# Layer 3 of a four-layer network: norm factors applied in pairs, disc units and spread statistics rescheduled, and a separate tail for the last image

## The chip, the cores and the metric

One core of a Trainium2 chip runs the whole network in one launch. The time is device microseconds (us) of that launch; three runs of the kernel before are known, and one further execution was recorded by the hardware profiler.

## What is computed

The input is `x`, 8 images of 32 x 32 tokens with 256 channels, float32. Four layers follow one another, each `x = x + f(group_norm(x))`. Only the fourth, layer 3, is touched (and one preparation step for it that is issued during layer 2):

```python
qkv = silu(x @ w_qkv.T); q, k, v = split(qkv, 3)
q, k = rope(rms_norm(q)), rope(rms_norm(k))          # per head, 8 heads of 32 channels
wp = silu(x @ w_wp.T + b_wp); width_raw, sharp_raw = split(wp, 2)
width = sigmoid(width_raw) * max_dist + 0.5; sharp = sigmoid(sharp_raw) * 9.5 + 0.5
scores = einsum(q, k_win) * 32**-0.5                 # a 7 x 7 window round each token
soft_mask = sigmoid((width - rel_dist) * sharp)      # the "soft disc"
attn = softmax(scores - (1 - soft_mask) * 10000)
out = rms_norm(einsum(attn, v_win), w_on)            # over all 256 channels
return silu((out + v) @ w_out.T)
```

(The rotation's angle depends on the head alone and is the same for q and k, so it cancels in the scores, and no rope step stands in the kernel.)

## The kernel before, in words

**Tiling.** Layer 3 works channel-major: 128 channels (four heads) in the partitions, the 1024 tokens of an image along the free axis. An image `b` has two channel halves `c`; one such half is a *chunk* `J = 2b + c`, 16 in all. A chunk is worked off in 8 *groups*, each two 8 x 8 blocks of queries against a window of 14 x 14 keys: 128 groups. The main loop (lines 2308 to 2333) runs over *steps* `n` from -4 to N + 2 with N = 128, and every step does one stage of several groups:

- `st.scores(n+3)`, TensorE (PE): 8 small matmuls into four PSUM tiles (L1692).
- `st.exps(n)`, ScalarE (ACT): four exponentials (L1715).
- `st.logits(n+3)`, VectorE (DVE): scores plus mask with the running minimum (L1705).
- `st.turn(n-2, i)`: PE transposes of the probabilities (L1733), DVE copies them out of PSUM (L1738).
- `soft(n+5)`, ACT: four tanh that make the soft disc (L2103); `masked(n+5)`, GpSimd (POOL): adds the hard window (L2110).
- `st.divide(n)`: reciprocal on DVE (L1722), product on POOL (L1723).
- `st.values(n-3)`: PE (L1749), then two DVE copies to the output tile `oT` (L1757).

**Order.** The order is written out by hand for PE, ACT, DVE and POOL (`manual_schedule`); each engine takes its instructions in that order, and SyncE (SP) issues the DMAs in it. All PSUM tiles come from one ring of 8 banks (`ring`, L1549), so a matmul into a new tile waits for the reader of the tile 8 places earlier.

**Fillers.** The rest of the layer is cut into units that `plan_chunk`, `plan_image` and the loop after L2251 give a due time in steps; `units(n)` emits those due, and `units(n + 0.5)` those of the half step. A unit may return a second part, kept in `later` and run by the next `finish()`. Due times relative to the chunk's first step 8J:

- `project` (L2042, silu with tanh at L2027): k at -12, -11.5, q at -11, -10.5, v at -7.5, -7. For k and q POOL squares the result (L2062).
- `roots` at -8: PE sums the squares of q and k per head, and for even J those of the attention output of image b - 2 (L2122, L2129), ACT loads another activation table (L2136) and takes Ln and Exp (L2137, L2138), which makes the reciprocal norm factors `fac[J]`; the next tanh loads the first table again.
- `head_scale` (L2144): one 32-row matmul spreads a factor over the channels, DVE multiplies (L2148); k at -6, -5.5, q at -5, -4.5.
- `in_strips` at -6 and `vturn` at -2, -1.5, -1, -0.5, 1.5: PE transposes v (L1766), ACT copies it from PSUM (L1771).

Relative to an image's first step 16b: statistics of the group norm at -23.5 to -22, `normed` at -13.5 and -13, `discs` (width and sharpness, L2075 to L2094, one chain over DVE and ACT) at -10 and -9.5; after the attention `tail_sq` (POOL, L2172) at 19 and 20, `tail_scale` (four 32-row matmuls, L2177, DVE L2181, POOL L2182) at 30 to 31.5, `output` (L2190, L2197, L2199, L2200) at 33.5, 39, 39.5 and 41.5, each with a `reload` of the residual three steps ahead. What is still due after the last step is emitted by the loop at L2334.

## Time and profile before

| what | us |
|---|---|
| three runs: median (lowest to highest) | 3300.57 (3299.59 to 3302.94) |
| the profiled execution: its time | 3305.0 |
| the profiled execution: span from first to last instruction | 3303.2 |
| layer 3 within the span: first projection to the end | about 2503 to 3303 |
| first exponential of group 0; of group 32; of group 112; end of the last | 2531.9; 2735.4; 3197.8; 3261.3 |
| last copy of an attention output (L1757) to the end of the span | 3272.95 to 3303.15 |

The span shares on the page are PE 96%, ACT 69%, DVE 66%, POOL 54% busy. "PEclk" is the clock granted to PE, 1.0 being full speed; "idle before" is what an engine waited ahead of an instruction, and the arrow names what ended the wait. A float32 matmul of the program appears as two PE instructions. L12 is line 12 of the kernel before.

### The profile page before, as it was taken

The page shows a single profiled execution, that of the slowest core. Times are in us where ns is not written, and L with a number is a line of the kernel's source. Part 1 is how long each engine was busy: PE and PEld are TensorE (multiplying, and loading weights), DVE is VectorE, ACT ScalarE, POOL GpSimd, SP SyncE. Part 2 cuts the span into 40 slices and gives each one's busy share as a digit, 9 for nine tenths or more (in the row PEclk, how much of TensorE's full clock was granted, in tenths as well). Part 3 has the DMA queues.
Part 4 walks back from the last instruction along what each step waited for, and adds up shares of the span by engine and source line. Part 5 has one row for each costly group of instructions (what it writes and reads, how often), then busy time and mean ns, then how long its engine had stood idle before and what let it go on. Part 6 is the DMA issues. An engine that isn't in the chain of part 4 may idle for free. (4 is left out here: it accounts for less than half of the span.)

```text
span 3303.2 us, 76346 instructions
## 1 busy us (share of the span) xinstructions
PE 3165.7 (96%) x30280; PEld 1638.2 (50%) x30280; DVE 2192.5 (66%) x5570; ACT 2278.5 (69%) x5066; POOL 1792.1 (54%) x1201
## 2 busy tenths in 40 slices
PE   7999999999998999899999999999998899999997
PEld 2323323323322444777777656666664555555554
DVE  4777777777785677565655546666664667777775
ACT  3667667667776567666555547677676878888885
POOL 4666666666663111344444445433436668788777
PEclk9999999999999999999999999999998879999999
DMA  3000000000011667787867630111111001110001
GB/s 142 1 26 10 17 26 1 26 26 1 26 39 57 235 233 260 208 206 204 182 192 205 182 138 28 66 41 40 53 55 44 2 14 40 34 37 30 27 27 62
DMA packets 139177, 267.92 MB, mean 81 GB/s; under 512 B 9218, under 2 KB 77700, under 8 KB 130500
## 3 DMA queue, kind: packets, MB, share of 16 engines
q1 hardware_dynamic: 132436, 242.67, 24.3%
q10 hardware_dynamic: 6384, 20.37, 1.8%
q8 instruction: 239, 3.92, 0.5%
q14 instruction: 118, 0.97, 0.1%
HBM read 177.81 MB, written 85.20 MB: 80 GB/s over the span
## 5 line engine op out<-in xcount | busy, mean ns | idle before, releaser
L694 DVE TENSOR_TENSOR e<-s,ret 128x1024 f32<-128x1024 f32 x512 | 602.1, 1217 | 174.4 <-PE s L688 171.9
L701 ACT ACTIVATE ea<-e 128x1024 f32<-128x1024 f32 x512 | 535.5, 1055 | 257.3 <-DVE e L694 234.9
L703 POOL TENSOR_TENSOR ea<-ea 128x1024 f32<-128x1024 f32 x128 | 304.1, 2376 | 284.9 <-ACT ea L701 216.9
L688 PE MATMUL s<-qk,qk 32*128 32x512 f32 x2048 | 302.1, 640 | 4.3 <-POOL qk L571 1.7
L1591 POOL TENSOR_TENSOR e<-e,su 128x616 f32<-128x616 f32 (+2 forms) x128 | 157.3, 1229 | 268.7 <-DVE su L1590 241.9
L740 PE MATMUL num<-e,v 128*32 128x512 f32 x2048 | 271.3, 595 | 0.0
L1738 DVE COPY pts<-pt 112x512 f32<-112x512 f32 x256 | 175.8, 687 | 137.5 <-PE pt L1733 135.7
L2103 ACT ACTIVATE e<-win,disc 128x196 f32<-128x196 f32 x512 | 239.5, 543 | 0.2
L1723 POOL TENSOR_TENSOR e<-e,su 128x784 f32<-128x784 f32 x128 | 191.4, 1495 | 87.9 <-DVE su L1722 62.0
L870 PE MATMUL up_ps<-x,wup 128*128 128x512 f32 x512 | 230.2, 604 | 4.0 <-POOL x L236 3.2
L1715 ACT ACTIVATE e<-e,mx 128x196 f32<-128x196 f32 x512 | 227.9, 453 | 0.0
L2110 POOL TENSOR_TENSOR e<-e,win 128x784 f32<-128x784 f32 x128 | 201.7, 1576 | 38.5 <-issue 31.6
L1282 POOL TENSOR_TENSOR decayed<-state,rb 128x520 f32<-128x520 f32 x48 | 50.8, 1058 | 304.2 <-PE sc L1215 112.7
L1586 ACT ACTIVATE e<-e,mx 128x154 f32<-128x154 f32 (+2 forms) x512 | 212.2, 425 | 0.0
L1086 ACT ACTIVATE d<-d,cols 128x128 f32<-128x128 f32 x512 | 163.9, 392 | 68.5 <-POOL d L1077 68.4
L713 PE MATMUL sm<-ea,ones 128*32 128x512 f32 x1536 | 208.8, 604 | 1.6 <-POOL ea L703 1.6
L897 DVE SCALAR_TENSOR_TENSOR cv<-xm,par,cv 128x512 f32<-128x512 f32 x192 | 144.7, 754 | 85.8 <-ACT cv L892 81.2
L2042 PE MATMUL qkv_ps<-xq,w 128*128 128x512 f32 x384 | 192.2, 627 | 1.2 <-ACT fac L2137 1.2
L1823 PE MATMUL qkv_ps<-x,w 128*128 128x512 f32 x384 | 182.7, 613 | 1.6 <-POOL x L236 1.6
L688 PEld LDWEIGHTS s<-qk,qk 32*128 32x128 f32 x2048 | 84.8, 182 | 197.2 <-issue 87.7
L1733 PEld LDWEIGHTS pt<-idg,e 128*112 128x112 f32 x1024 | 121.5, 140 | 122.5 <-issue 91.0
L1733 PE MATMUL pt<-idg,e 128*112 128x128 f32 x1024 | 166.5, 289 | 8.4 <-DVE oT L1757 3.1
(245 smaller groups left out, 6932.8 us busy)
## 6 DMA issues: line engine op xcount, KB each, us to landing
d<-l1rows SPq DMA_DIRECT2D x64, 512.0 KB
x<-x SPq DMA_DIRECT2D x25, 1024.0 KB
l1xm<-xm SPq DMA_DIRECT2D x16, 1024.0 KB
l1sz<-sz SPq DMA_DIRECT2D x16, 1024.0 KB
xv<-l1xm SPq DMA_DIRECT2D x32, 512.0 KB
l1xa<-xa SPq DMA_DIRECT2D x16, 1024.0 KB
xa<-l1xa SPq DMA_DIRECT2D x16, 1024.0 KB
rb<-l1rows SPq DMA_DIRECT2D x32, 512.0 KB
```

The source lines that it names most:

```text
L688: nc.tensor.matmul(s[:, j % 2], qk[b, 1, c][g, kb * P : (kb + 1) * P], qk[b, 0, c][g, h * HALF : (h + 1) * HALF], start=True, stop=True,)
L694: nc.vector.tensor_mul(e[n, i], s, m)
L701: nc.scalar.activation(ea[n, i], e[n, i], AF.Abs)
L703: nc.gpsimd.tensor_add(ea[n, i], ea[n, i], ea.pop((n - 1, i)))
L713: nc.tensor.matmul(acc["sm"][g, :], ones, two[j // 2][:, j % 2, :], start=kb == 0 and k == 0, stop=kb == 4 and k == 2,)
L740: nc.tensor.matmul(acc["num"][g, :], v[b][:, kb, vc], e[n, j // 2][:, j % 2, :], start=kb == 0, stop=kb == 7,)
L870: nc.tensor.matmul(ps, wup[:, kc, m * P : (m + 1) * P], seg(s)[:, kc], start=kc == 0, stop=kc == 1,)
L1586: self.nc.scalar.activation(p[:, j], p[:, j], AF.Exp, scale=-1.0, bias=mx[:, j : j + 1], accum_out=su[:, j : j + 1],)
L1715: self.nc.scalar.activation(e[:, j], e[:, j], AF.Exp, scale=-1.0, bias=mx[:, j : j + 1], accum_out=self.su[:, j : j + 1],)
L1733: self.nc.tensor.transpose(ps[: self.PART, at : at + P], self.tile(n)[:, 2 * i + j, k * self.PART : (k + 1) * self.PART], self.K.ident,)
L2103: nc.scalar.activation(e[:, j], win[:, 0], AF.Tanh, scale=disc[b][:, i, 8 + h : 9 + h], bias=disc[b][:, i, h : h + 1],)
L2110: nc.gpsimd.tensor_add(e, e, win[:, 1].unsqueeze(1).to_broadcast([P, 4, NWIN]))
```

## The change

All in layer 3:

- `head_scale` does both halves of k, or of q, in one unit: two 32-row matmuls one after the other into two PSUM tiles, the two products in the second part. Due at -6 (k) and -5 (q).
- `tail_scale` has one matmul per token half where it had one per half and channel half: the matrix of the matmul is now ones, and the weight `w_on` goes in as the per-partition scalar of the DVE instruction. Due at 27.5 and 28.5. Its constants come by two DMAs in the preparation step.
- The copy of the transposed v (`value_unit`) goes from ACT to DVE and into the second part.
- `discs` becomes a chain of five parts, one per `finish()`; due at -13, -12.5. `finish()` runs one part of every chain. `normed` at -15, statistics at -23.75 (two), -22.5, -21.5.
- v is projected at -8.5 and -8; `roots` comes after it in the same step.
- `exps(n+1)` stands where `exps(n)` stood. In every eighth step (`rooted`) `soft(n+5)` comes ahead of the units, and a `finish()` and a quarter step follow the logits.
- `output` runs by token half at 29.5, 30.5, 31, 31.5, and `reload` at 26.5, 27.5, 28, 30.5.
- The last image has a tail of its own (`last_tail`, due N + 3): PSUM takes `wo` times v first and `wo` times the normed output is added to it there, so no POOL addition of v; half of the squares are taken on ACT; the residual is the image itself, loaded whole at 16b + 6.

```diff
-        self.nc.scalar.copy(
+        return lambda: self.nc.vector.tensor_copy(
...
+        def root(ps, n):
+            r = wk.tile([P, HALF], F32, name="fac", bufs=2)
+            nc.scalar.preload_act_table_set("natural_log_exp_and_others")
+            nc.scalar.activation(r[:n], ps[:n], AF.Ln, bias=eps[:n])
+            nc.scalar.activation(r[:n], r[:n], AF.Exp, scale=-0.5)
+            return r
...
-        def head_scale(J, s, h):
-            g = slice(32 * (2 * s + h), 32 * (2 * s + h) + 32)
-            ps = st.ring("fac_ps")
-            nc.tensor.matmul(ps, spread[g, s], fac[J][g], start=True, stop=True)
+        def head_scale(J, s):
+            ps = [st.ring("fac_ps") for _ in range(2)]
+            for h in range(2):
+                g = slice(32 * (2 * s + h), 32 * (2 * s + h) + 32)
+                nc.tensor.matmul(ps[h], spread[g, s], fac[J][g], start=True, stop=True)
...
-            nc.tensor.matmul(ps, won[g, c], fac[J][g], start=True, stop=True)
+            nc.tensor.matmul(ps, ones[g], fac[J][g], start=True, stop=True)
             def rest():
-                d = st.o[b, c][:, hs]
-                nc.vector.tensor_mul(d, d, ps)
-                nc.gpsimd.tensor_add(d, d, vT[b, c][:, hs])
+                for c in range(2):
+                    d = st.o[b, c][:, hs]
+                    nc.vector.scalar_tensor_tensor(
+                        d, d, on[:, c : c + 1], ps, ALU.mult, ALU.mult)
+                    nc.gpsimd.tensor_add(d, d, vT[b, c][:, hs])
...
+        def last_tail(b):
+            ps = {}
+            def early(m):
+                for h in range(2):
+                    ps[m, h] = st.ring("out_ps")
+                    for kc in range(2):
+                        nc.tensor.matmul(ps[m, h], wo[:, kc, m * P : (m + 1) * P],
+                            vT[b, kc][:, h * HALF : (h + 1) * HALF],
+                            start=kc == 0, stop=False)
+            early(0)
+            sq, o = sqs["o", 1], st.o[b, 1]
+            nc.scalar.activation(sq[:, HALF:], o[:, HALF:], AF.Square)
+            sums = st.ring("ms_ps")
+            for c, h in ((0, 0), (0, 1), (1, 0), (1, 1)):
+                if c and h:
+                    early(1)
+                nc.tensor.matmul(sums[32 * h : 32 * h + 32], sel[:, 32:64], ...)
+            f = root(sums, 64)
+            for h in range(2):
+                fp = st.ring("fac_ps")
+                nc.tensor.matmul(fp, ones[g], f[g], start=True, stop=True)
+                for c in range(2):
+                    nc.vector.scalar_tensor_tensor(d, d, on[:, c : c + 1], fp, ALU.mult, ALU.mult)
+            for h in range(2):
+                for m in range(2):
+                    for kc in range(2):
+                        nc.tensor.matmul(ps[m, h], wo[...], st.o[b, kc][:, hs],
+                            start=False, stop=kc == 1)
+                    y = half_silu(p)
+                    nc.vector.scalar_tensor_tensor(y, y, 1.0, p, ALU.add, ALU.mult)
+                    e = nc.vector if m and h else nc.gpsimd
+                    e.tensor_add(r, r, y)       # r is the image, loaded again at 16b + 6
+                    nc.sync.dma_start(dst[...], r)
...
-                if 0 <= n < N:
-                    st.exps(n)
+                if 0 <= n + 1 < N:
+                    st.exps(n + 1)
+                rooted = n % 8 == 0
+                if rooted and 1 < n + 5 < N:
+                    soft(n + 5)
                 units(n)
                 if 0 <= n + 3 < N:
                     st.logits(n + 3)
+                if rooted:
+                    finish()
+                    units(n + 0.25)
                 if 0 <= n - 2 < N:
                     st.turn(n - 2, 0)
                 finish()
-                if 1 < n + 5 < N:
+                if not rooted and 1 < n + 5 < N:
                     soft(n + 5)
...
         def finish():
-            while later:
-                later.pop(0)()
+            due = later[:]
+            later[:] = [r for r in [f() for f in due] if callable(r)]
```

More of the change, by code (lines that the diff above doesn't have):

```diff
@@ L90, in shape_constants @@
     k["k_spread"] = (p[:, None] % 32 == p[None] // 32).astype(f)
+    k["k_one8"] = np.tile(p[:, None] % 32 == 8, (1, P)).astype(f)
     return {n: np.ascontiguousarray(v) for n, v in k.items()}
@@ L145, in layouts @@
     )
-    a["l3_on"] = i["L3_conv_w_on"].reshape(2, P)
+    a["l3_on"] = _cols(i["L3_conv_w_on"])
     a.update(shape_constants())
@@ L395, in factors @@
             )
-            nc.vector.memset(won, 0.0)
         def weight():
-            for h in range(2):
-                nc.sync.dma_start(
-                    self.won[32 * h + 8 : 32 * h + 9], a["l3_on"].unsqueeze(0)
-                )
+            nc.sync.dma_start(self.won[:, 0], a["k_one8"])
+            nc.sync.dma_start(self.won[:, 1, 0:2], a["l3_on"])
         return [loads, factors, weight]
@@ L1671, in __init__ @@
         super().__init__(K, wk, pp, pairs, n_img, ebufs)
-        self.slots, self.s = 20, {}
+        self.slots, self.s, self.su = 20, {}, {}
         shape = [P, 4, 2 * self.PART]
@@ L1712, in exps @@
         mx, e = self.mx.pop(n), self.prob(n)
-        self.su = self.wk.tile([P, 4], F32, name="su", bufs=4)
+        su = self.su[n] = self.wk.tile([P, 4], F32, name="su", bufs=4)
         for j in range(4):
@@ L1716, in exps @@
                 e[:, j], e[:, j], AF.Exp, scale=-1.0, bias=mx[:, j : j + 1],
-                accum_out=self.su[:, j : j + 1],
+                accum_out=su[:, j : j + 1],
             )
     def divide(self, n):
-        e = self.prob(n)
-        self.nc.vector.reciprocal(self.su, self.su)
-        self.nc.gpsimd.tensor_mul(e, e, self.su.unsqueeze(2).to_broadcast([P, 4, NWIN]))
+        e, su = self.prob(n), self.su.pop(n)
+        self.nc.vector.reciprocal(su, su)
+        self.nc.gpsimd.tensor_mul(e, e, su.unsqueeze(2).to_broadcast([P, 4, NWIN]))
     def turn(self, n, i):
@@ L1997, in layer3 @@
         K.ring = st.ring
-        bwp, sel, spread, won = first.bwp, first.sel, first.spread, first.won
+        bwp, sel, spread = first.bwp, first.sel, first.spread
+        ones, on = first.won[:, 0], first.won[:, 1, 0:2]
         wo, win, eps = first.wo, first.win, first.eps
@@ L2085, in rest, with silu, silu2, sigmoid @@
                 )
-                th = wk.tile([P, 4, 16], F32, name="dth")
-                nc.scalar.activation(th, d, AF.Tanh)
+                return silu
+            def silu():
+                th = wk.tile([P, 4, 16], F32, name="dth", bufs=2)
+                nc.scalar.activation(th, disc[b][:, 4 * u : 4 * u + 4, :], AF.Tanh)
+                return lambda: silu2(th)
+            def silu2(th):
+                d = disc[b][:, 4 * u : 4 * u + 4, :]
                 nc.vector.scalar_tensor_tensor(d, th, 1.0, d, ALU.add, ALU.mult)
+                return sigmoid
+            def sigmoid():
+                d = disc[b][:, 4 * u : 4 * u + 4, :]
                 nc.scalar.activation(d, d, AF.Tanh, scale=0.5)
+                return scales
+            def scales():
+                d = disc[b][:, 4 * u : 4 * u + 4, :]
                 wd, sp = d[:, :, 0:8], d[:, :, 8:16]
@@ L2133, in roots @@
                         )
-            n = P if heads else 64
-            r = wk.tile([P, HALF], F32, name="fac", bufs=2)
-            nc.scalar.preload_act_table_set("natural_log_exp_and_others")
-            nc.scalar.activation(r[:n], ps[:n], AF.Ln, bias=eps[:n])
-            nc.scalar.activation(r[:n], r[:n], AF.Exp, scale=-0.5)
-            fac[J] = r
-        def head_scale(J, s, h):
-            g = slice(32 * (2 * s + h), 32 * (2 * s + h) + 32)
-            ps = st.ring("fac_ps")
-            nc.tensor.matmul(ps, spread[g, s], fac[J][g], start=True, stop=True)
+            fac[J] = root(ps, P if heads else 64)
+        def head_scale(J, s):
[3 more added lines that the diff above has]
+                nc.tensor.matmul(ps[h], spread[g, s], fac[J][g], start=True, stop=True)
             def rest():
-                d = dest(J, s, h)
-                nc.vector.tensor_mul(d, d, part(ps))
+                for h in range(2):
+                    d = dest(J, s, h)
+                    nc.vector.tensor_mul(d, d, part(ps[h]))
             return rest
@@ L2166, in vturn, with tail_sq, tail_scale @@
                 st.v[b, c] = wk.tile([P, st.slots, P], F32, name="v", bufs=2)
-            st.value_unit(strips, st.v[b, c], u)
-        def tail_sq(b, c):
+            return st.value_unit(strips, st.v[b, c], u)
+        def tail_sq(b, c, n=L):
             sqs["o", c] = wk.tile([P, L], F32, name="sq", bufs=4)
-            nc.gpsimd.tensor_mul(sqs["o", c], st.o[b, c], st.o[b, c])
-        def tail_scale(J, b, c, h):
+            o = st.o[b, c][:, 0:n]
+            nc.gpsimd.tensor_mul(sqs["o", c][:, 0:n], o, o)
+        def tail_scale(J, b, h):
             g, hs = slice(32 * h, 32 * h + 32), slice(h * HALF, (h + 1) * HALF)
             ps = st.ring("fac_ps")
-            nc.tensor.matmul(ps, won[g, c], fac[J][g], start=True, stop=True)
+            nc.tensor.matmul(ps, ones[g], fac[J][g], start=True, stop=True)
             def rest():
-                d = st.o[b, c][:, hs]
-                nc.vector.tensor_mul(d, d, ps)
-                nc.gpsimd.tensor_add(d, d, vT[b, c][:, hs])
+                for c in range(2):
+                    d = st.o[b, c][:, hs]
+                    nc.vector.scalar_tensor_tensor(
+                        d, d, on[:, c : c + 1], ps, ALU.mult, ALU.mult
+                    )
+                    nc.gpsimd.tensor_add(d, d, vT[b, c][:, hs])
             return rest
@@ L2208, in reload @@
             nc.sync.dma_start(r, src[:, m, b * L + h * HALF : b * L + (h + 1) * HALF])
+        def last_tail(b):
[4 more added lines that the diff above has]
+                    for kc in range(2):
+                        nc.tensor.matmul(
+                            ps[m, h], wo[:, kc, m * P : (m + 1) * P],
+                            vT[b, kc][:, h * HALF : (h + 1) * HALF],
+                            start=kc == 0, stop=False,
+                        )
+            early(0)
[5 more added lines that the diff above has]
+                    early(1)
+                nc.tensor.matmul(
+                    sums[32 * h : 32 * h + 32], sel[:, 32:64],
+                    sqs["o", c][:, h * HALF : (h + 1) * HALF],
+                    start=c == 0, stop=c == 1, skip_group_check=True,
+                )
+            f = root(sums, 64)
+            for h in range(2):
+                hs = slice(h * HALF, (h + 1) * HALF)
+                fp = st.ring("fac_ps")
+                g = slice(32 * h, 32 * h + 32)
+                nc.tensor.matmul(fp, ones[g], f[g], start=True, stop=True)
+                for c in range(2):
+                    d = st.o[b, c][:, hs]
+                    nc.vector.scalar_tensor_tensor(
+                        d, d, on[:, c : c + 1], fp, ALU.mult, ALU.mult
+                    )
+            for h in range(2):
+                hs = slice(h * HALF, (h + 1) * HALF)
+                for m in range(2):
+                    p = ps[m, h]
+                    for kc in range(2):
+                        nc.tensor.matmul(
+                            p, wo[:, kc, m * P : (m + 1) * P], st.o[b, kc][:, hs],
+                            start=False, stop=kc == 1,
+                        )
+                    y = half_silu(p)
+                    nc.vector.scalar_tensor_tensor(y, y, 1.0, p, ALU.add, ALU.mult)
+                    r = x[b][:, m, hs]
+                    e = nc.vector if m and h else nc.gpsimd
+                    e.tensor_add(r, r, y)
+                    nc.sync.dma_start(
+                        dst[:, m, b * L + h * HALF : b * L + (h + 1) * HALF], r
+                    )
@@ L2219, in plan_chunk @@
                 fill.add(n - 12 + i / 2, lambda s=s, h=h: project(J, s, h))
-                fill.add(n - 6 + i / 2, lambda s=s, h=h: head_scale(J, s, h))
-            fill.add(n - 7.5, lambda: project(J, 2, 0))
-            fill.add(n - 7, lambda: project(J, 2, 1))
+            for s in range(2):
+                fill.add(n - 5 - s, lambda s=s: head_scale(J, s))
+            fill.add(n - 8.5, lambda: project(J, 2, 0))
+            fill.add(n - 8, lambda: project(J, 2, 1))
             fill.add(n - 6, lambda: in_strips(J))
@@ L2228, in plan_image @@
                 fill.add(n - 27.5, lambda: load(b))
+                ahead = (n - 23.75, n - 23.75, n - 22.5, n - 21.5)
                 for i in range(4):
                     fill.add(
-                        max(n - 23.5, -3) + i / 2,
+                        ahead[i] if b > 1 else -3 + i / 2,
                         lambda i=i: gn.stats(b, image_parts(x[b]), i),
@@ L2236, in plan_image @@
                 for c in range(2):
-                    fill.add(n - 13.5 + c / 2, lambda c=c: normed(b, c))
+                    fill.add(max(n - 15, 2) + c / 2, lambda c=c: normed(b, c))
                 for u in range(2):
-                    fill.add(n - 10 + u / 2, lambda u=u: discs(b, u))
+                    fill.add(max(n - 13, 4) + u / 2, lambda u=u: discs(b, u))
+            if b == n_img - 1:
+                fill.add(n + 6, lambda: load(b))
+                fill.add(n + 11, lambda: tail_sq(b, 0))
+                fill.add(N + 1.75, lambda: tail_sq(b, 1, HALF))
+                fill.add(N + 3, lambda: last_tail(b))
+                return
             for c in range(2):
                 fill.add(n + 19 + c, lambda c=c: tail_sq(b, c))
-                for h in range(2):
-                    fill.add(
-                        n + 30 + c + h / 2,
-                        lambda c=c, h=h: tail_scale(2 * b + 4, b, c, h),
-                    )
-            for i in range(4):
-                at = n + 32 + (1.5, 7, 7.5, 9.5)[i]
-                fill.add(at - 3, lambda i=i: reload(b, i // 2, i % 2))
-                fill.add(at, lambda i=i: output(b, i // 2, i % 2))
-        for J in range(2 * n_img + 3):
+                fill.add(n + 27.5 + c, lambda c=c: tail_scale(2 * b + 4, b, c))
+            for i in range(4):
+                h, m = divmod(i, 2)
+                fill.add(n + (26.5, 27.5, 28, 30.5)[i], lambda h=h, m=m: reload(b, m, h))
+                fill.add(n + (29.5, 30.5, 31, 31.5)[i], lambda h=h, m=m: output(b, m, h))
+        N = len(st.groups)
+        for J in range(2 * n_img + 1):
             b, c = divmod(J, 2)
             t = b - 2 if c == 0 and b >= 2 else None
+            if J < 2 * n_img:
+                plan_chunk(J)
             if J and (J < 2 * n_img or t is not None):
                 fill.add(8 * J - 8, lambda J=J, t=t: roots(J, t))
-            if J < 2 * n_img:
-                plan_chunk(J)
         for b in range(n_img):
@@ L2264, in layer3 @@
                 fill.add(at, lambda J=J, u=u: vturn(J, u))
-        N = len(st.groups)
         later = []
@@ L2274, in finish, with all_of @@
         def finish():
-            while later:
-                later.pop(0)()
+            due = later[:]
+            later[:] = [r for r in [f() for f in due] if callable(r)]
+        def all_of(*rests):
+            while rests:
+                rests = [r for r in [f() for f in rests] if callable(r)]
         def start():
@@ L2281, in start @@
             rest = [discs(0, 0), discs(0, 1), project(0, 1, 0)]
-            rest[0]()
-            rest[2]()
-            r = project(0, 1, 1)
-            rest[1]()
-            r()
+            all_of(rest[0], rest[2])
+            all_of(rest[1], project(0, 1, 1))
             soft(0)
@@ L2296, in start @@
             in_strips(0)
-            for i in range(4):
-                head_scale(0, 1 - i // 2, i % 2)()
+            for s in (1, 0):
+                head_scale(0, s)()
             masked(1)
@@ L2333, in layer3 @@
                     masked(n + 5)
+                if n == N + 1:
+                    units(N + 1.75)
             for n in range(N + 3, N + 32):
```

## The prediction

> **What bounds the kernel now.** I read first the busy time by chunk of eight groups, cut at the first exponential of every eighth group. Columns: the stretch and its length; busy time and instructions of PE, weight load, DVE, ACT, POOL; the granted clock; DMA.

> ```profile
> 2582.20:2631.40 49.20, 45.59 (x450) 24.93 (x449) 32.44 (x131) 37.78 (x112) 30.38 (x23) 0.79 0.01 2
> 2828.00:2875.60 47.60, 45.34 (x528) 26.59 (x516) 35.04 (x135) 42.39 (x121) 38.66 (x29) 1.00 0.11 35
> 2875.60:2919.20 43.60, 43.35 (x444) 23.04 (x448) 34.31 (x134) 38.60 (x114) 35.40 (x28) 1.00 0.12 38
> 3101.50:3155.00 53.50, 51.50 (x524) 28.98 (x513) 34.90 (x135) 42.49 (x122) 38.77 (x29) 0.87 0.04 12
> 3259.60:3303.20 43.60, 32.14 (x207) 14.24 (x206) 17.07 (x37) 10.57 (x22) 27.35 (x21) 0.87 0.24 79
> ```

> In the middle of layer 3 (steps 32 to 111, ten chunks, 2735.4 to 3197.8) PE is the bound: 45.3 + 43.4 = 88.7 busy of 91.2 us per image, ACT at 81, DVE at 69, POOL at 74. The first four chunks have less work on every engine and yet take 203.5 us, 50.9 each, because the clock is at 0.8. The last stretch is a chain with nothing beside it.

> Second, the groups by line in the three images from 2783 to 3058 (count, busy, mean ns, idle before):

> ```profile
> L1738 DVE COPY pts<-pt 112x512 f32<-112x512 f32 x96 | 66.0, 688 | 44.6 <-PE pt L1733 43.6
> L2144 PE MATMUL fac_ps<-fac,spread 32*128 32x512 f32 x48 | 26.9, 640 | 0.6 <-ACT v L1771 0.5
> L1771 ACT COPY v<-vt 112x512 f32<-112x512 f32 x31 | 17.8, 574 | 8.5 <-PE vt L1766 8.5
> L2177 PE MATMUL fac_ps<-fac,won 32*128 32x512 f32 x24 | 13.4, 640 | 0.0
> ```

> The factors cost PE 9.0 (L2144) and 4.5 us (L2177) per image. Third, PE's timeline, at the start of the layer and in the middle:

> ```profile
> 2512.17 1.14 PE L2144 MATMUL fac_ps<-fac,spread 32*128 32x512 f32 x8 [1.98 <-ACT fac L2138]
> ...
> 2980.00 1.12 PE L2144 MATMUL fac_ps<-fac,spread 32*128 32x512 f32 x2
> 2981.05 0.65 PE L1733 MATMUL pt<-idg,e 128*112 128x128 f32 x4
> 2981.63 1.12 PE L2144 MATMUL fac_ps<-fac,spread 32*128 32x512 f32 x2
> ```

> At the start four calls (eight instructions, four different groups of 32 rows) stand back to back and take 1.14 us together. In the middle a call stands alone and holds PE 1.05 us. So neighbours on different rows run side by side.

> Fourth, the timeline behind a `roots`:

> ```profile
> 2586.74 1.28 ACT L2103 ACT_TABLE_LOAD   x1
> 2588.04 1.87 ACT L2103 ACTIVATE e<-win,disc 128x196 f32<-128x196 f32 x4
> 2589.82 0.57 ACT L2027 ACTIVATE th<-qkv_ps 128x512 f32<-128x512 f32 x1
> 2590.42 0.75 DVE L2054 SCALAR_TENSOR_TENSOR vT<-th,qkv_ps 128x256 f32<-128x256 f32 x2 [4.97 <-ACT th L2027]
> ```

> The tanh of v, due half a step after `roots`, waits behind a table load and the soft disc, and DVE stands 4.97 us at the head of its queue with all logits and copies behind it. Fifth, stretches cut at the clock's changes:

> ```profile
> 2588.80:2592.21 3.41, 0.89 (x8) 0.84 (x8) 1.75 (x7) 3.41 (x13) 1.57 (x1) 1.00 0.00 0
> 2592.21:2612.69 20.48, 20.26 (x150) 9.71 (x149) 14.64 (x61) 11.51 (x38) 10.72 (x8) 0.50 0.00 1
> ...
> 2800.45:2803.86 3.41, 3.39 (x25) 1.35 (x12) 3.41 (x15) 3.41 (x13) 3.35 (x4) 1.00 0.26 82
> 2803.86:2807.28 3.42, 3.42 (x45) 2.21 (x46) 3.23 (x14) 1.15 (x6) 2.98 (x3) 0.50 0.00 1
> ```

> The first stall leaves PE 0.89 us of work in 3.41, and 20.48 us at half clock follow. But after 2800.45 the clock halves although PE was busy for 3.39: 2.24 of that were lone 32-row factor matmuls, which use a quarter of the rows.

> [...]

> **The change, part by part.** Ten middle chunks first.

> *Paired `head_scale`.* Four lone calls per chunk become two pairs: 2 x 1.05 = 2.1 us less PE. Two switches between kinds of matmul go too: PE's starts show about 0.08 each way, 0.3 per chunk. Ten chunks: -24.

> *`tail_scale`.* Four calls per image become two, -2.1, and -0.2 for switches; five images: -11. On DVE four products of 0.68 stay four; POOL keeps its four additions.

> *Roots, v earlier, soft disc first.* The same four table loads per image (1.28 each), but no DVE part waits behind them: the tanh of v is ahead of `roots` on ACT. In the middle chunks the v parts wait 14.3 / 3 = 4.8 us per image on DVE, of which PE's idle rows (L2190 5.0, L2122 1.9, for three images) show 2.3 reaching PE. Five images: -11; bound from both sides -20 and 0. The half clock at 3117 to 3131 (the 53.5 against 47.6) may go: -6 to 0, I take -3.

> *The v copies.* Ten per image leave ACT (-5.7) and come to DVE at the price of L1738, 0.69, or 0.61 from start to start: DVE goes from 69 to 75 per image, PE to about 82. As an average that is hidden. It is not hidden in place: at steps 8 to 11 of an image PE has little (start to start 15 us by my sum), while DVE holds logits, copies, statistics (4 x 0.67), factor products (6 x 0.68), v products: 19 us. A ring of 8 banks lets it lag by some 3. I give back 1 to 5 us per image; take 2.5: +13.

> [...]

> *Clock.* Steps 1, 2 and 9 to 11 now hold no 128-row projection or output. Before, an output stood at 1.5 and 9.5. Weighing each matmul's streaming time by its rows x columns over 128 x 128, I estimate the array's share in use at about 0.4 to 0.5 there; the windows ahead of a fall show 0.22 and 0.29, one that did not fall (2984.78) 0.34. Bounds: none, or 5 to 8 us per chunk (53.5 - 47.6 = 5.9). I take one image in three: 5 x 0.35 x 6 = +10.

> *`discs` in five parts, `exps` a step ahead:* ACT waited 6.4 + 2.1 us in three images inside the disc chain, DVE 3.8; neither is the bound. `exps(n+1)` needs logits issued two steps before; nothing new is late. The four image statistics come with a lead of over 20 steps. Nothing, -5 to +5.

> *`reload` at 30.5* needs a buffer that the store of the output at 29.5 frees; SP stands there some 3 us (a store takes about 2.8), the stores of 30.5 and 31 behind it, and POOL's last addition waits. Up to 1 us, hidden; without cover +5.

> Middle: -24 - 11 - 11 - 3 + 13 + 10 = **-26** (PE's relief is 35 of it).

> *First four chunks* (203.5 us). The half clock there starts in the stall behind `roots` or with lone factors; both are cut. ACT then has about 37 us per chunk (41 and 38 less 2.9), PE at full clock 36. I take 43.5, leaving room for the clock to fall in half of them: 4 x (43.5 - 50.9) = **-30**. Bounds: 39 (-47) and 50.9 (0).

> *Steps 112 to 127*: tail work of image 6 moves in, projections have ended, ACT (exponentials 1.77, discs 1.88 a step) rules: **-3**, -6 to +2.

> *Drain.* Now the last exponential ends at 3261.3, the last `oT` copy at 3272.95, because 8 L2177, 16 L2190 and four POOL additions of image 6 stand between; these are due before step 128 now. Without them: product 1.5, transposes 1.0, copies 1.3, values 0.65, copy 0.35, about 5 instead of 11.6: -6. From that copy to the end it takes 30.2. New: PE 16 early instructions at 0.43 = 6.9, sums 2.7, Ln and Exp 1.5, ones 1.1, first product 0.7, 16 output instructions 6.9, tanh 0.6, product 0.7, add 0.7, store to end 2.8 = 24.6; plus 2 for a half clock behind the Ln: 26.6, so -3.6. Together **-10** (-14 to -3).

> *Preparation* (two DMAs for two, a memset less, in layer 2): nothing.

> Sum: -26 - 30 - 3 - 10 = -69 against the span of 3303.2 and its execution's 3305.0; that execution is 4.4 above the median of 3300.57, which shifts alike. 3300.6 - 69 = 3231.6; I round to **3235**.

> **Rivals.** *A: PE's relief is eaten in place.* Middle chunks give nothing (DVE in steps 8 to 11 and ACT behind the tables bind, sum +26), the early chunks 24, the rest 10: 3300 - 34 = 3266, range 3262 to 3294. For it: ACT is already at 42.4 of 47.6. Against: DVE's 43.6 us of waiting for transposes shows that it follows PE. Chance 0.20. *B: all arrives*: early chunks at 39, middle at PE's full relief with no fall: -47 - 49 - 13: 3190, between 3175 and 3205; 0.13 (0.02 below). *C, slower: the gate falls in every chunk.* Place: steps 1 to 3 and 9 to 11. Half clock doubles 9 us of PE work there; of that some 2 are hidden. At 8 per chunk: ten middle chunks +80 - 46 (the PE relief and the roots), early chunks unchanged, drain -8: about 3327. It decides for slower from about 5.5 us per middle chunk (6 for more than 0.2%). 0.10. *D: no difference* (within 0.2%, 3294 to 3307, about what a measurement of this kernel can tell from no change): gate and relief cancel; 0.05.

> My forecast, 3205 to 3265, has 0.50. Faster: 0.50 + 0.20 + 0.15 = 0.85; same 0.05; slower 0.10. The range reaches from B's middle to A's end, 3180 to 3292.

> **What would show it.** Right: the matmuls of `head_scale` in fours within 1.1 us; four instructions of `tail_scale` per image; no DVE wait over 2 us on L2054; middle chunks at 41 to 46; clock near 1.0 from 2532 on; last `oT` copy some 5 us behind the last exponential. Wrong: a clock of 0.8 to 0.9 in middle chunks (C); DVE's wait for transposes gone and PE idle behind DVE copies (A).

## The result, and the profile after

The changed kernel takes **3262.86 us** (median of four runs, 3257.78 to 3264.23) against 3301.76 of the kernel before on the same chip: ratio 0.9881, 95% interval 0.9865 to 0.9896. That is -39 where the forecast said -66. The profiled execution is the fastest of the four (3257.8, span 3256.0). The two profiled executions are 47 us apart, 4 of it ahead of layer 3 and 43 in the parts below.

Cut by the last `oT` copy of a group, from before to after: from the first projection of layer 3 to group 0: 59.3 to 51.3 us; groups 0 to 31: 196.2 to 174.2; groups 32 to 111: 462.5 to 450.8; groups 112 to 127: 57.0 to 57.3; from the last copy to the end: 30.3 to 28.3. The start gained what was forecast: by the forecast's own cut, at the first exponentials of groups 0 and 32, the first four chunks went from 203.5 to 175.1 us, -28 for -30. The middle gained 12 of 26, the end 2 of 13.

First view, as in the prediction: busy time by chunk of the kernel after, cut at the first exponential of every eighth group (stretch and its length; PE, weight load, DVE, ACT, POOL; granted clock; DMA).

```profile
2521.90:2562.70 40.80, 37.05 (x373) 21.86 (x372) 30.02 (x127) 38.22 (x113) 29.34 (x23) 0.96 0.09 28
2562.70:2608.20 45.50, 41.10 (x440) 23.53 (x448) 38.33 (x141) 35.61 (x108) 30.50 (x24) 0.85 0.01 1
2608.20:2646.40 38.20, 36.40 (x444) 22.36 (x435) 33.51 (x123) 38.11 (x114) 31.58 (x23) 1.00 0.10 30
2646.40:2697.00 50.60, 48.57 (x476) 26.79 (x476) 42.39 (x154) 36.76 (x109) 39.08 (x31) 0.87 0.01 2
...
2784.10:2826.80 42.70, 40.92 (x480) 24.85 (x478) 35.21 (x126) 39.42 (x116) 37.49 (x27) 1.00 0.24 76
2826.80:2877.40 50.60, 49.02 (x475) 27.41 (x476) 41.70 (x154) 36.83 (x110) 38.45 (x31) 0.87 0.01 2
...
3105.30:3148.10 42.80, 42.67 (x471) 23.29 (x469) 36.50 (x139) 36.60 (x109) 37.62 (x30) 1.00 0.01 2
...
3214.20:3256.00 41.80, 34.31 (x230) 16.08 (x220) 15.94 (x36) 10.41 (x20) 15.51 (x13) 0.89 0.16 58
```

The first four chunks took 49 to 55 us at clocks of 0.76 to 0.85. They now take 40.8, 45.5, 38.2 and 50.6 at 0.96, 0.85, 1.00 and 0.87: only the third has its full clock, and the fourth takes longer than before (49.0). In the middle the even chunks went from 47.6 to 42.7. But three odd middle chunks take 49.4 to 50.6 where they took 43.5, at a clock of 0.87 to 0.90. Where the clock holds, an odd chunk takes 42.8 or 44.4. So the expected gain did come in the even chunks and was given back in the odd ones.

Second view, groups by line in three images (2784.1 to 3062.6): count, busy, mean ns, idle before.

```profile
L1737 DVE COPY pts<-pt 112x512 f32<-112x512 f32 x96 | 65.3, 680 | 39.3 <-PE pt L1732 38.6
L1770 DVE COPY v<-vt 112x512 f32<-112x512 f32 x31 | 21.1, 679 | 0.0
L1765 PE MATMUL vt<-idg,strips 128*112 128x128 f32 x120 | 20.4, 297 | 8.5 <-DVE qT L2052 8.3
L2109 DVE SCALAR_TENSOR_TENSOR disc<-disc 128x32 f32<-128x32 f32 x6 | 7.6, 1269 | 0.2
L2107 DVE TENSOR_SCALAR disc<-disc 128x32 f32<-128x32 f32 x6 | 4.3, 722 | 0.0
L2108 DVE TENSOR_SCALAR disc<-disc 128x32 f32<-128x32 f32 x6 | 3.8, 628 | 0.0
```

and the same three disc instructions in the kernel before:

```profile
L2094 DVE SCALAR_TENSOR_TENSOR disc<-disc 128x32 f32<-128x32 f32 x6 | 1.1, 192 | 0.2
L2092 DVE TENSOR_SCALAR disc<-disc 128x32 f32<-128x32 f32 x6 | 1.1, 182 | 1.9 <-ACT disc L2089 1.9
L2093 DVE TENSOR_SCALAR disc<-disc 128x32 f32<-128x32 f32 x6 | 1.0, 174 | 0.0
```

DVE's wait for transposes stays (38.6, was 43.6), but PE has a new wait, 8.3 us for DVE's `qT`, and the three small disc instructions have grown from 0.18 to between 0.63 and 1.27 us. The timeline of one image's two disc units (start, duration, engine):

```profile
2817.31 2.51 POOL L2193 TENSOR_TENSOR sq<-oT 128x1024 f32<-128x1024 f32 x1
2817.86 0.22 DVE L2095 SCALAR_TENSOR_TENSOR disc<-dth,disc 128x64 f32<-128x64 f32 x1
...
2820.81 1.49 POOL L1722 TENSOR_TENSOR e<-e,su 128x784 f32<-128x784 f32 x1
2821.31 1.03 DVE L2107 TENSOR_SCALAR disc<-disc 128x32 f32<-128x32 f32 x1
...
2824.84 1.08 DVE L2108 TENSOR_SCALAR disc<-disc 128x32 f32<-128x32 f32 x1
2824.84 1.04 POOL L2062 TENSOR_TENSOR sq<-qT 128x512 f32<-128x512 f32 x1
...
2825.84 1.50 POOL L1722 TENSOR_TENSOR e<-e,su 128x784 f32<-128x784 f32 x1
2825.95 1.43 DVE L2109 SCALAR_TENSOR_TENSOR disc<-disc 128x32 f32<-128x32 f32 x1
...
2827.31 0.68 DVE L2052 SCALAR_TENSOR_TENSOR qT<-th,qkv_ps 128x512 f32<-128x512 f32 x1
...
2828.04 1.10 PE L1765 MATMUL vt<-idg,strips 128*112 128x128 f32 x4 [2.61 <-DVE qT L2052]
```

Each long one of the three ends 0.04 to 0.05 us behind a POOL instruction: 2821.31 + 1.03 = 2822.34 against 2820.81 + 1.49 = 2822.30, and so on. In the kernel before, from 2760 to 2960, these three always started while POOL ran nothing. Behind them DVE's `qT` product stands in the queue, and PE idles 2.61 us for it. It is not always DVE that pays. `silu2` (L2095) took 0.22 us in the middle of a POOL instruction, but there POOL took longer: from 2600 to 3180 the six POOL squares (L2193) with an L2095 in them took 2.51 us and the eight others 1.89 to 1.91; the additions of the hard window (L2125) took 1.92 to 2.11 with one and 1.57 to 1.61 without. Why they hold each other up, and what decides which of the two stands, is not shown.

Third view, stretches cut at the clock's changes:

```profile
2823.60:2827.00 3.40, 1.59 (x24) 0.81 (x8) 3.37 (x6) 3.40 (x13) 3.40 (x3) 1.00 0.00 0
2827.00:2833.80 6.80, 5.76 (x57) 4.66 (x58) 6.28 (x27) 3.44 (x12) 5.93 (x5) 0.50 0.01 2
2850.90:2854.30 3.40, 3.06 (x12) 1.44 (x12) 3.37 (x16) 3.40 (x13) 3.34 (x4) 1.00 0.01 2
2854.30:2861.10 6.80, 6.80 (x50) 3.22 (x49) 5.59 (x21) 3.06 (x11) 5.04 (x5) 0.50 0.01 2
```

The stall leaves PE 1.59 us of work in a window of 3.41, and 6.8 us at half clock follow. A second fall comes 27 us later behind a window in which PE was busy for 3.06 us, with factors and few other matmuls. By my weighing (streaming time x rows x columns over 128 x 128, from the matmul records) the share of the array in use was 0.26 in both. Over the layer, half clock went from 120.5 us to 91.1.

Fourth view, a pair of `head_scale` matmuls (PE, and the weight loads PEld):

```profile
2846.77 0.29 PEld L2163 LDWEIGHTS fac_ps<-fac,spread 32*128 32x128 f32 x2 [0.29 <-issue]
2846.77 1.93 PE L2163 MATMUL fac_ps<-fac,spread 32*128 32x512 f32 x4
...
2847.58 0.29 PEld L2163 LDWEIGHTS fac_ps<-fac,spread 32*128 32x128 f32 x2 [0.52 <-DVE pts L1737]
```

The two matmuls do not run side by side. The second one's weight load stands 0.52 us for a DVE copy: its PSUM bank, the second that the pair takes from the ring, is not free yet. In the middle chunks nearly all pairs take 1.43, 1.72 or 1.93 us, not the 1.14 of the group at the layer's start, which waited for no bank.

### The profile page after: what moved, and what is told of

It reads as the page before. It is cut to its first block, busy times and chain, and to the rows that moved or that the text cites. A ratio compares the mean times of both kernels' runs of the same rounds, so it can differ in the third digit from the quotient of the medians.

```text
span 3256.0 us, 76392 instructions
## 1 busy us (share of the span) xinstructions
PE 3124.6 (96%) x30264; PEld 1631.6 (50%) x30264; DVE 2248.7 (69%) x5650; ACT 2240.0 (69%) x4987; POOL 1792.3 (55%) x1196
## 4 chain that ended last, share of the span: by engine, by line
PE 38%; ACT 8%; DVE 4%; POOL 4%; issue 3%; DMA 1%; ACTq 0%; SPq 0%; POOLq 0%; DVEq 0%
PE qkv_ps L1822 5%; PE qkv_ps L2042 4%; PE pt L1604 3%; PE dn_ps L1349 2%; PE pt L1732 2%; PE pr_ps L1882 2%; PE o L1623 2%; PE s L1564 2%; PE out_ps L2215 2%; PE vt L1649 1%; ACT e L2118 1%; ACT e L1714 1%; PE sc L1214 1%; PE num_ps L1239 1%; PE vt_ps L1125 1%
## 5 line engine op out<-in xcount | busy, mean ns | idle before, releaser
L1737 DVE COPY pts<-pt 112x512 f32<-112x512 f32 x256 | 173.7, 679 | 88.6 <-PE pt L1732 86.9
L2125 POOL TENSOR_TENSOR e<-e,win 128x784 f32<-128x784 f32 x128 | 205.1, 1603 | 25.7 <-ACT e L2118 17.9
L1281 POOL TENSOR_TENSOR decayed<-state,rb 128x520 f32<-128x520 f32 x48 | 50.9, 1060 | 303.0 <-PE sc L1214 69.1
L1704 DVE CUSTOM_DVE_ANT_0 e<-s,e 128x196 f32<-128x196 f32 x512 | 153.6, 355 | 12.8 <-POOL e L2125 11.3
```

## The experiments

Times are medians; the ratio is to the kernel before, timed on the same chip with its 95% interval. Small differences between two medians need care: what lies ahead of layer 3 is the same code in every variant of the kernel after, and took between 2491.4 and 2498.5 us in their profiled executions. Where it matters, the layer's own time is given: from the first projection to the end of the profiled execution.

### Is it the disc instructions beside POOL?

**e1_scales_pool**: the three instructions go to POOL itself.

```diff
-nc.vector.tensor_scalar(wd, wd, md / 2, md / 2 + 0.5, ALU.mult, ALU.add)
-nc.vector.tensor_scalar(sp, sp, 9.5 / 4, 10.5 / 4, ALU.mult, ALU.add)
-nc.vector.scalar_tensor_tensor(wd, wd, -1.0, sp, ALU.mult, ALU.mult)
+nc.gpsimd.tensor_scalar(wd, wd, -md / 2, -md / 2 - 0.5, ALU.mult, ALU.add)
+nc.gpsimd.tensor_scalar(sp, sp, 9.5 / 4, 10.5 / 4, ALU.mult, ALU.add)
+nc.gpsimd.tensor_mul(wd, wd, sp)
```

> The changed kernel, with the last part of the disc chain (two scalings and a product on 128x32) on POOL instead of DVE. Theory G (clock): in the changed kernel these three DVE instructions take up to 1.0 to 1.5 us each instead of 0.17 to 0.19 (a POOL instruction runs beside each long one), DVE's product for q stands behind them, PE idles up to 2.6 us and the clock halves for 6.8 us at the turn to chunks 7, 9 and 11. Without them the falls at 2827, 2919 and 3015 go and those chunks lose 5 to 7 us each, with something in the early images: 3235 to 3248 against 3262.9. Rival V (DVE is the bound because it took over the copies of v): 1 to 3 us less at most, falls stay. Rival S (the falls come from the steps without 128-row matmuls): the falls stay, no change within 5.

Measured: 3238.51, ratio 0.9814 (0.9795 to 0.9832), 24 us under the kernel after. On POOL the three take 0.22, 0.22 and 0.25 us, and PE no longer waits for `qT`. Two odd chunks of this kernel, with and without a fall of the clock:

```profile
2815.30:2859.80 44.50, 43.22 (x438) 22.94 (x428) 38.03 (x141) 36.92 (x109) 38.72 (x33) 1.00 0.01 2
2859.80:2902.50 42.70, 42.53 (x526) 26.55 (x524) 34.13 (x131) 39.43 (x115) 37.42 (x30) 1.00 0.24 76
2902.50:2950.00 47.50, 46.24 (x438) 24.13 (x428) 38.09 (x141) 36.95 (x109) 39.60 (x34) 0.93 0.01 2
```

First and third line are odd chunks: 44.5 at full clock, 47.5 with one fall of 6.8 us. So a fall of 6.8 us costs 3 us here. That these three instructions, on DVE and at this place, cost 24 us is shown. Most of it goes by the clock: half clock is 54.6 us here, 91.1 in the kernel after, which at 3 us per 6.8 makes 16 us (an estimate).

### What is the pairing of the factors worth?

**e3_unpaired**: the kernel after, `head_scale` in four units of one matmul.

```diff
-for s in range(2):
-    fill.add(n - 5 - s, lambda s=s: head_scale(J, s))
+for i in range(4):
+    s, h = 1 - i // 2, i % 2
+    fill.add(n - 6 + i / 2, lambda s=s, h=h: head_scale(J, s, h))
```

> The changed kernel with the factor matmuls one at a time, due at -6, -5.5, -5, -4.5 as before. If PE's relief counts in full, 2.4 us per chunk in 15 chunks are lost: 3290 to 3300. Theory G: the pairs stand in steps that PE does not bound, so only part shows directly (0 to 1 per chunk), but lone quarter-row matmuls bring more half clock: 3270 to 3295. If pairing were worth nothing: 3258 to 3266.

Measured: 3261.72, 0.9883 (0.9861 to 0.9905). The time is that of the kernel after, but the clock is not: half clock is 58.0 us here and 91.1 there. So the equal times do not say by themselves that pairing does nothing in this kernel; e10_pool_unpaired below is the cleaner comparison.

**e6_before_paired**: the reverse edit on the kernel before, and nothing else.

> The kernel before, with nothing changed but the pairing of the four head_scale matmuls (two units of two matmuls at steps -5 and -6 in place of four units of one). The prediction's term: 2.4 us of PE work less per chunk in fifteen chunks, where PE was thought to bind, so 24 us in the ten middle chunks and up to 12 more before and after: 3267 to 3279, and no window at half clock at 2803.9. Theory P (the steps with head_scale are not bound by PE, pairing is worth nothing in any kernel, as in e3_unpaired): 3296 to 3303. A time between 3282 and 3294 says that pairing was worth something while the values' copies and the soft disc still stood where they were, and lost its worth by the rest of the change.

Measured: 3262.65, 0.9875 (0.9853 to 0.9896): pairing alone brings 40 us, as much as the whole change, more than either theory gave. Theory P falls for this kernel. By chunk, the third, seventh and thirteenth:

```profile
2614.90:2660.20 45.30, 39.44 (x469) 24.26 (x471) 31.54 (x125) 40.96 (x118) 33.73 (x25) 0.96 0.08 25
2792.00:2839.70 47.70, 43.97 (x528) 26.56 (x516) 35.98 (x135) 42.43 (x121) 38.77 (x29) 1.00 0.11 35
3063.10:3108.70 45.60, 43.44 (x512) 26.39 (x504) 35.11 (x134) 42.53 (x121) 37.77 (x28) 1.00 0.04 13
```

They took 55.0, 47.6 and 53.5. Most of the gain is clock: half clock in layer 3 falls from 120.5 us to 41.9. Between the profiled executions (48 us apart) 24 lie in groups 0 to 31, 8 ahead of them (3 of these ahead of the layer), and 16 in the middle, of which 8 are the chunk that had the long fall. The stalls that start a fall are still there (a share of 0.12 at 2578.5, half clock at 2581.9); but before, the clock then stayed down for 14 to 24 us, in windows of lone quarter-row matmuls with shares of 0.34 to 0.61 (2592.2 to 2609.3), and now it is back after 3.4, behind shares of 0.75 and 0.77. Pairing shortens the falls; in the middle PE's own relief is at most the other 8 us.

**e10_pool_unpaired**: e1_scales_pool with the edit of e3_unpaired.

> e1_scales_pool without the pairing of head_scale (four lone matmuls per chunk at -6, -5.5, -5, -4.5). By the prediction's term, with PE the bound again now that the stall is gone: 2.4 us for each of fifteen chunks on top of 3238.5, so 3270 to 3276. By the clock (pairing is worth what it keeps of full clock, and the half clock of the kernel before came from the stall behind the roots, which this kernel no longer has): 3236 to 3246.

Measured: 3240.32, 0.9806 (0.9774 to 0.9838), against 3238.51: no difference that can be told. With the stall gone, PE's term still does not appear. Two unpaired matmuls take 2 x 1.13 = 2.26 us there, pairs 1.67 in the mean. Half clock is alike (47.8 us, 54.6 in e1_scales_pool), and the two chunks of a middle image without a fall take 44.1 + 42.8 = 86.9 us unpaired and 42.7 + 44.5 = 87.2 paired.

### Is it the share of the array that moves the clock?

**e7_dense**: the kernel after, with one unread matmul of 128 rows x 128 columns x 512 added to every odd chunk.

```diff
+def dense():
+    ps = st.ring("dense_ps")
+    nc.tensor.matmul(ps, w[:, 0, 0:P], w[:, 0, 0:HALF], start=True, stop=True)
+
+for J in range(1, 2 * n_img, 2):
+    fill.add(8 * J + 2.5, dense)
```

> The kernel after with work added: in each odd chunk, at step 2.5, one matmul of 128 rows x 128 columns x 512 that nobody reads (0.86 us at full clock). Theory K (the clock falls after a 3.41-us window in which the array's share is under a third, and each fall of 6.8 us costs about 3 us): the falls at 2854.3 and 2946.5 go, four to five falls fewer in the layer, and the kernel is the same or faster in spite of the added work: 3245 to 3262. Theory W (the clock falls because PE waits, whatever it does; the added matmul is only more work): the falls stay, and 7 x 0.9 us on top: 3263 to 3275.

Measured: 3246.10, 0.9826 (0.9809 to 0.9843): 17 us faster with more work. The second fall is gone from all middle chunks, and half clock goes from 91.1 us to 53.5.

**e12_sparse**: the same, but with 32 rows x 32 columns.

```diff
-    nc.tensor.matmul(ps, w[:, 0, 0:P], w[:, 0, 0:HALF], start=True, stop=True)
+    nc.tensor.matmul(ps[:32], w[0:32, 0, 0:32], w[0:32, 0, 0:HALF], start=True, stop=True)
```

> Control to e7_dense: the kernel after with an unread matmul at the same steps, but of 32 rows x 32 columns x 512, which streams as long and uses a sixteenth of the array. If it is the share of the array that keeps the clock, the falls stay as in the kernel after and the time is 3260 to 3270. If e7_dense gained because PE was busy there at all, or because the units behind it moved, this gains as much: 3243 to 3250.

Measured: 3257.01, 0.9852 (0.9826 to 0.9878): 11 us slower than with the full matmul (9 by the ratios, whose intervals overlap), though both stream 0.6 us per instruction; 6 faster than the kernel after, which theory K did not expect. Two of its windows at steps 2 to 3 of a chunk:

```profile
2671.10:2674.50 3.40, 3.40 (x26) 1.12 (x10) 3.40 (x14) 3.39 (x12) 2.93 (x3) 1.00 0.01 2
2852.00:2855.40 3.40, 3.40 (x14) 1.24 (x12) 3.40 (x15) 3.40 (x13) 2.94 (x3) 1.00 0.01 2
```

PE is busy for all of both. Behind the first (share 0.27) the clock fell, behind the second (0.33) it held. In three kernels (after, e7_dense, e12_sparse), from 2600 to 3200, the clock fell behind every full-clock window with a share up to 0.32 and behind none with 0.33 or more, among them one of e12_sparse that held at 2831.5 with PE busy 0.59 of the time and a share of 0.35.

The other runs show no such line. The kernel before fell behind a window of 0.34 (3114.5) and held behind one of 0.31 (2892.6); e11_pool_sums_first_dense, below, fell behind 0.35 (2922.7); e6_before_paired held behind 0.29 (3035.9) and e13_pool_old_order behind five of 0.30. So by this estimate, from records of which a few can be missing, both occur between 0.29 and 0.35.

Nor does the control part the theories in the middle chunks: the three second falls of the kernel after (shares 0.26, 0.31, 0.31) are gone with the small matmul too (0.33, 0.34, 0.38). It was set too near the shares at which both occur: a sixteenth more, or a shift of the units, was enough, and which of them is not shown. By the layer's own time e12_sparse is 9 us behind e7_dense, 7 of it in groups 0 to 31. That busy time alone does not decide is shown by the windows; that the share does is argued, from shares that are my estimate. They sort most of these rows, not all.

### The values' copies and the order around the roots

**e2_v_on_act**: the kernel after, the copies of v back on ACT and in the first part of their unit.

```diff
-return lambda: self.nc.vector.tensor_copy(
+self.nc.scalar.copy(
```

> The changed kernel with the copies of the transposed v back on ACT and in the first part of the unit. Rival V: DVE gets 6.9 us per image back, the middle odd chunks (47 by the last output copy) come to 43 to 44: 3245 to 3255. Theory G: the copies are not what PE waits for; ACT takes 2.9 per chunk more and delays soft discs: 3260 to 3280, the falls of the clock stay.

Measured: 3272.00, 0.9911 (0.9894 to 0.9928): 9 slower. PE's longest waits in it, from 2600 to 3180 (total, times, longest), and DVE's for the tanh of v:

```profile
PE s L1691 <- ACT v L1770: 13.9, 7, 2.2
PE vt L1765 <- DVE qT L2052: 10.6, 6, 1.9
```

```profile
DVE vT L2054 <- ACT th L2027: 18.7, 14, 2.4
```

With the copies on ACT, PE waits 13.9 us for them, which the kernel after's waits do not show, and the tanh of v comes late to DVE (4.9 us of waiting there in the kernel after).

**e13_pool_old_order**: e1_scales_pool with the roots ahead of v, v's projections a step later and the soft disc always behind the turn.

```diff
-rooted = n % 8 == 0
+rooted = False
...
-fill.add(n - 8.5, lambda: project(J, 2, 0))
-fill.add(n - 8, lambda: project(J, 2, 1))
+fill.add(n - 7.5, lambda: project(J, 2, 0))
+fill.add(n - 7, lambda: project(J, 2, 1))
```

(and `roots` added ahead of `plan_chunk`).

> e1_scales_pool with the former order around the roots: the projections of the values at -7.5 and -7, the roots ahead of them in their step, the soft disc behind the first turn in every step. By the prediction's term (the values' DVE part stands 5 us behind a table load and the soft disc; -11 in the layer for curing it): 3238.5 + 11 = 3250, with the clock falling behind the stall up to 3265. If the new order is worth nothing: 3234 to 3243.

Measured: 3251.39, 0.9837 (0.9812 to 0.9863), 13 slower than e1_scales_pool (8 by the ratios, whose intervals overlap a little). The layer's own time is 13 longer as well: 8 in groups 0 to 31, 8 in groups 32 to 111, 3 less in the rest. DVE's wait for the tanh of v, first with the old order, then in e1_scales_pool:

```profile
DVE vT L2054 <- ACT th L2027: 27.0, 13, 3.1
```

```profile
DVE vT L2054 <- ACT th L2027: 2.0, 7, 0.5
```

### The last image

**e4_old_tail**: the kernel after, the last image through the ordinary tail.

```diff
-if b == n_img - 1:
+if False:
...
-for J in range(2 * n_img + 1):
+for J in range(2 * n_img + 3):
```

> The changed kernel without the last image's own tail: image 7 goes through squares, roots, scale and outputs like the others, after the last step. The prediction priced the new tail from the last output copy on at 3.6 us: 3266 to 3268 here. The profile after shows 28.3 us from the last output copy to the end against 30.2 before: 3263 to 3268. If the tail is worth more than it shows (POOL additions and table loads in a row): up to 3275.

Measured: 3252.76, 0.9851 (0.9835 to 0.9867), 10 faster than with `last_tail`. Between the profiled executions it is 5, nearly all from group 112 on (57.3 + 28.3 against 54.7 + 26.3). PE at the end of the kernel after, and ACT's wait:

```profile
3227.22 3.70 PE L2244 MATMUL out_ps<-vT,wo 128*128 128x512 f32 x8
...
3232.69 3.70 PE L2244 MATMUL out_ps<-vT,wo 128*128 128x512 f32 x8
...
3236.32 1.04 PE L2257 MATMUL ms_ps<-sq,sel 128*32 128x512 f32 x2
3237.40 0.68 ACT L2132 ACTIVATE fac<-ms_ps,eps 64x512 f32<-64x512 f32 x1 [7.74 <-PE ms_ps L2257]
```

The early matmuls of the values, meant to be out of the way, stand ahead of the sums on PE; the sums end 10.1 us after the last values, 3.8 in e4_old_tail.

**e9_pool_sums_first**: e1_scales_pool, in `last_tail` the sums first, `early(0)` and `early(1)` behind the call of `root`.

> e1_scales_pool with one order changed in last_tail: PE does the four sums first and the eight early matmuls of the values behind them, while ACT takes the roots. If the early matmuls' place is what makes last_tail slow (sums 10.1 us behind the last values, 3.5 in the old tail), the sums end 6 us sooner and the matmuls hide behind Ln, Exp and the table load: 3238.5 - 6 = 3232 (3229 to 3235). If the output matmuls then wait for the early ones, or the half clock takes it, 3236 to 3241.

Measured: 3233.14, 0.9788 (0.9769 to 0.9808), 5 under e1_scales_pool, 4 by the layer's own time; from the last `oT` copy to the end 22.9 us against 27.0:

```profile
3208.73 2.09 PE L2254 MATMUL ms_ps<-sq,sel 128*32 128x512 f32 x6
3210.75 7.13 PE L2244 MATMUL out_ps<-vT,wo 128*128 128x512 f32 x16
3217.81 1.13 PE L2266 MATMUL fac_ps<-fac,won 32*128 32x512 f32 x4
```

The early matmuls now fill the time of the roots, and at full clock.

**e8_pool_old_tail**: e1_scales_pool and e4_old_tail together.

> e1_scales_pool and e4_old_tail together: the disc scales on POOL, and the last image through the ordinary tail. If the two causes are apart (middle and end), the gains add: 3262.9 - 24 - 10 = 3229 (3224 to 3234). If the old tail's gain came in the middle chunks through the same stall (last image's units at other steps), 3236 to 3241.

Measured: 3237.47, 0.9806 (0.9782 to 0.983). By the medians a miss: 1 us under e1_scales_pool where 10 were expected. In the profiled executions the end is shorter by 4.3 us (groups 112 on, 81.1 against 85.4), which is what e4_old_tail's profile shows (81.0 against 85.6), and the part of the layer ahead of it takes the same (653.3 against 653.5). There the gains do add; the layer began 7 us later in this execution (2498.4 against 2491.4), behind code that is the same in both. Whether the old tail is worth the 5 us of the profiles or the 10 of e4_old_tail's median, these runs do not tell.

### The best of these

**e11_pool_sums_first_dense**: e9_pool_sums_first with `dense` of e7_dense.

> e9_pool_sums_first with the unread 128 x 128 x 512 matmul in each odd chunk at step 2.5. e9 has two falls left in the middle, behind windows with a share of 0.26 (at 2751.5 and two chunks pairs later), 3 us each. Clock theory: both go, -6, and five to seven matmuls of 0.6 to 1.0 us cost 0 to 4: 3227 to 3233. More work and nothing else: 3234 to 3240.

Measured: 3228.03, 0.9768 (0.9742 to 0.9794): 77 us under the kernel before on that chip, 35 under the kernel after. Half clock in the layer is 23.9 us. Of the two falls that were to go, one did; the other is half as long (3.4 us at 2926.1).

## Why the prediction was right and wrong

**Right: the first four chunks** (-30, measured -28), and the step behind it that lone factors and the stall behind the roots hold the clock down. e6_before_paired shows that either half of the cure is enough: pairing alone (-24 in groups 0 to 31), and the kernel after without pairing (172.6 us there against 174.2 with it). They are not two gains to be added.

**Right: roots, v earlier, soft disc first** (-11): by e13_pool_old_order 8 us in the middle, for which the term was meant, and 8 more in the first four chunks. It was tried only in the kernel without the disc stall. The sign set for it holds too: in the kernel after no DVE wait on L2054 is over 0.7 us.

**Wrong: paired `head_scale`, -24.** The step said that two lone calls of 1.05 us become one pair of 1.1. The price came from the row of four at the start, where no bank was awaited. In the middle the pair waits for its second bank and takes 1.67, against 2.26 for two lone ones: 0.6 saved per pair, 1.2 per chunk, 12 in ten chunks. Not even that was felt: 86.9 us per image without pairs, 87.2 with them (e10_pool_unpaired). PE "busy 45.3 of 47.6" is not PE bound: its work had room to stretch. The sign set for this step, "in fours within 1.1 us", is denied by the profile.

**Wrong in sign: the v copies, +13.** I weighed where DVE is crowded and not what ACT's copies held up, for which PE waits 13.9 us in e2_v_on_act: -9 by that run.

**Wrong: `discs` in five parts, "nothing, -5 to +5".** This is the step that cost the forecast: +24 by e1_scales_pool. I asked which engine the parts wait for and not what runs beside them. The chain before ran its three small DVE instructions while POOL idled; its fourth, L2088, already showed 0.99 us for work of 0.2 (the same instruction, L2095, took 0.21 to 0.22 us in the kernel after), and I read past that row.

**Clock, +10: right in one of two places.** The prediction looked for falls at steps 1 to 3 and 9 to 11 of an image. Three odd middle chunks lost 5 to 6 us each (49.4 to 50.6 against 44.4), about +17, with two falls in each. The second falls (2854.3, 2946.5, 3038.6) come at steps 10 to 11, as foreseen. The first (2827.0, 2919.2, 3014.7) come at steps 5 to 7, behind the disc stall, which was not foreseen, and in the middle chunks none comes at steps 1 to 3. Without the stall the first falls vanish, and two of the second kind remain, 3 us each: +6 (e1_scales_pool).

**The end, -13; measured -2.** Two terms failed. The -6 for image 6's tail work: it was moved into the last eight groups, which take 26.9 us where they took 20.7, and its outputs (L2215) still stand among the last transposes; the last `oT` copy comes 11.9 us behind the last exponential, not 5. And the sum from there to the end: it counted the 16 early instructions as 6.9 us ahead of the sums without asking whether they had to stand there; e9_pool_sums_first gets 4 back by their place alone. The output matmuls were partly at half clock (10.13 us for 16 instructions, 7.13 in e9_pool_sums_first), for which I had taken 2.

Sum: without the disc stall the change would be at e1's 3238.5, next to the 3235 forecast (whose terms add to 3231.6), but by other terms: pairing 24 less, copies 22 more, the end 11 less, the first chunks 12 more (53.1 + 160.4 in e1 against 59.3 + 196.2 before, forecast -30). Rival A (relief eaten in place, 3266) is nearest in number, not in mechanism: DVE did hold PE in one place of the odd chunks, by three small instructions that took up to 1.51 us beside POOL and not by its load. Rival C's fall (its "gate" is the granted clock) came in odd chunks only. So it is in part luck that the measured time lies within the stated range: single terms were off by 11 to 24 us, both ways, and largely cancelled.

What stays open: how much `tail_scale`'s shorter form is worth by itself, which was not tried; what decides whether DVE or POOL stands when they meet; what the old tail is worth, 5 or 10 us; and whether it is the share of the array that moves the clock, or something that goes with it.

## To carry to other kernels

Small DVE instructions on SBUF operands took 0.17 to 0.19 us here while POOL ran nothing and up to 1.51 beside a POOL instruction, and all that was behind them in DVE's queue stood with them (PE idled 2.61 us for it): when such work is moved, look at what POOL does at its new place, or give it to POOL (24 us less in e1_scales_pool). Two packed matmuls that waited for their second bank took 1.43 to 1.93 us here, four that waited for no bank 1.14; and a PE busy for 45.3 of 47.6 us was no proof that PE binds (86.9 us per image without pairs, 87.2 with them): try the relief alone. When a clock's fall is what costs, do not add up two cures of the same fall: pairing brought 40 us in the kernel before and none that can be told here with the stall gone (e10_pool_unpaired). And a little more dense work in the thin place was cheaper here than none (17 us in e7_dense).
